# Two adjacency products as pairs of 64-row matmuls into two PSUM banks

## The chip, the cores and the metric

The kernel runs on one core of a Trainium2 chip. The metric is the device time of one execution in microseconds. Three runs of the kernel before are the base: 1310.28, 1312.41 and 1313.22 us, median 1312.41.

## What is computed

Four graph layers act one after the other on x, which has 8 batches, 2048 nodes and 64 features (f32). Each ends in `x = layernorm(x + layer(x))` over the 64 features. All of them use one adjacency matrix `adj` of 2048 x 2048, which is a symmetric 0/1 pattern whose rows are divided by their sums. The change touches the last two layers:

```python
# layer 2
out_self = jnp.einsum('bni,io->bno', x, weight_self)
x_neighbors = jnp.einsum('nm,bmi->bni', adj, x)
out_neighbors = jnp.einsum('bni,io->bno', x_neighbors, weight_neighbor)
return out_self + out_neighbors + bias
# layer 3
A_td = A + jnp.eye(n, dtype=A.dtype)
deg = jnp.sum(A_td, axis=1)
dinv = jax.lax.rsqrt(deg)
A_hat = dinv[:, None] * A_td * dinv[None, :]
H = jnp.einsum('bmd,nm->bnd', X, A_hat)
X_p = jnp.einsum('bnd,kd->bnk', H, W)
return X_p
```

Layer 0 is a polynomial in `adj` with weights of each node's own. Layer 1 mixes an adjacency product with attention over 64 groups.

## The kernel before

The 2048 nodes are 16 tiles of 128 partitions (NT = 16, P = 128). A row of a node holds all batches and features, 8 x 64 = 512 columns (BC). Since `adj` is a pattern times a scale of each row, layer 0 writes the pattern as exact zeros and ones ("masks") to DRAM, one block of 1 MB for each tile of output nodes. `cols_of` holds the scales for each node: `s1` for layer 2 and `sdinv` for layer 3.

**A product.** An adjacency product of output tile j is 16 steps over the input tiles mt, each with the mask block as the stationary operand (128 rows by 128 columns) and 512 columns of input as the moving operand. The input is split in two, a high and a low part, each of which goes through TensorE in the one-pass type fp32r; so a step is two matmuls, and a tile is 32, all accumulated in one PSUM bank. `times_mask` (L1440, its matmul on L1442) issues the two matmuls of a step. `mask_tile` (L1434) loads a mask block by a DMA on SP's queue (L1437); the pool has three buffers (L1504).

**Layer 2** (loop on L1545). Layer 1 leaves the projected inputs as `y_hi` and `y_lo`, and x with the self term in `x2`. For each tile j:

- 32 matmuls into `acc` (L1547 to L1549), whose pool `acc2` has two buffers (L1506);
- `r = acc * s1 + x2` on VectorE, one `scalar_tensor_tensor` (L1551);
- the layer norm of r (helper `layernorm`, L132 to L155: two reductions and two more passes over 512 columns on VectorE, a square and a square root on ScalarE), whose result goes back into `x2`;
- for tile j - 1, `projected` (L1528): four 128 x 128 transposes on TensorE (`transpose`, L167, tile `tr_l` in the profile), their copy `xT` on VectorE (L1518), four plain f32 matmuls with W (L1532, tile `yp`), then `v_hi` on ScalarE (L1536), and `v_lo` and a new `x2` on VectorE (L1537, L1540).

**Layer 3** (loop on L1558). The same product with `v_hi` and `v_lo`, `r = acc * sdinv + x2` (L1564), the layer norm, and the output's DMA on ScalarE's queue (L1569).

**PSUM.** In these layers the pools are `acc2`, `tr2` and `mm2`, of two buffers each, one bank a buffer.

**What sets the order of the work.** In layers 0 and 1 the order on each engine is the order of the code: these parts stand in `program_order()` (L210). Layers 2 and 3 do not. There a scheduler, which works with estimated durations and takes the code's order as priority, orders the instructions of each engine when the program is built. In the profile of before one sees its work: the 32 products of a tile stand on TensorE as five ahead of `yp` and 27 behind it, though the code has `projected` between two whole products. On the chip each engine then takes its instructions in that order.

**64-row matmuls elsewhere.** Several places already use pairs of 64-row matmuls on partitions 0 to 63 and 64 to 127, with plain f32 operands: L1109 (tile `pp`, layer 0), L807 (`fc`, layer 1) and L872 (`u`, the projection that prepares layer 2). A plain f32 matmul appears in the profile as two instructions, an fp32r one as one.

Of the kernel before, what the change touches and what calls it, by code (L numbers as in the profile page):

```python
# [8 lines left out]
F32 = mybir.dt.float32  # L9
# [3 lines left out]
ALU = mybir.AluOpType  # L13
# [5 lines left out]
P = 128  # L19
NT = N // P  # L20
NQ, QW = 4, 512
NP = B // 2
BC = B * C
# [34 lines left out]
def r_(ap):  # L58
    return ap.bitcast(F32R)
# [3 lines left out]
def kernel(  # L63
# [28 lines left out]
    nc = tc.nc  # L92
# [18 lines left out]
    cols_of = {  # L111
        k: const.tile([P, NT], F32, tag=k, name=k)
        for k in ("s1", "s2", "sdeg", "dinv", "dinv2", "sdinv")
    }

    def buffer(pool, k, name, per=1):

        return Tiles(
            [pool.tile([P, BC], F32, tag=f"b{k}_{t}", name=f"{name}_{t}") for t in range(NT)], per
        )  # L120
# [11 lines left out]
    def layernorm(ln, r, dst, name, swap=False, mhalf=None):  # L132

        r3 = b_view(r)
        s = ln([P, B], "s", f"s_{name}")
        nc.vector.tensor_reduce(s, r3, AX.X, ALU.add)
        nc.vector.scalar_tensor_tensor(
            r3, bcast(s), -1.0 / C, r3, op0=ALU.mult, op1=ALU.add  # L140
        )
        sq = ln([P, BC], "sq", f"sq_{name}")
        nc.scalar.activation(sq, r, AF.Square, scale=C ** -0.5)
        var = ln([P, B], "var", f"var_{name}")
        nc.vector.tensor_reduce(var, b_view(sq), AX.X, ALU.add)
        rstd = ln([P, B], "rstd", f"rstd_{name}")
        if mhalf is not None:
            nc.vector.tensor_scalar(var, var, EPS, None, op0=ALU.add)
            nc.gpsimd.tensor_tensor(rstd, var, mhalf, ALU.pow)
        else:  # L150
            std = ln([P, B], "std", f"std_{name}")
            nc.scalar.activation(std, var, AF.Sqrt, bias=eps_t)
            nc.vector.reciprocal(rstd, std)
        if not swap:
            nc.vector.tensor_tensor(b_view(dst), r3, bcast(rstd), ALU.mult)  # L155
            return
        for bq in range(2):
            nc.vector.tensor_tensor(
                swapped(dst, bq),
                r[:, 4 * bq * C:4 * (bq + 1) * C].rearrange("p (h l c) -> p h l c", h=2, l=2),  # L160
                rstd[:, 4 * bq:4 * bq + 4].rearrange("p (h l o) -> p h l o", h=2, o=1)
                .to_broadcast([P, 2, 2, C]),
                ALU.mult,
            )

    def transpose(dst, src):
        nc.tensor.matmul(dst, src, ident, start=True, stop=True, is_transpose=True)  # L167
# [1214 lines left out]
    def short_program(top):  # L1382
# [49 lines left out]
        y_hi, y_lo = buffer(big, 0, "y_hi"), buffer(big, 1, "y_lo")  # L1432

        def mask_tile(pool, j, name):  # L1434

            a = pool.tile([P, NT, P], F32, tag="mj", name=f"mj_{name}_{j}")
            nc.sync.dma_start(a, masks[j])  # L1437
            return a

        def times_mask(acc, a, hi, lo, mt):  # L1440
            for part in (hi, lo):
                nc.tensor.matmul(  # L1442
                    acc, r_(a[:, mt, :]), r_(part[:, mt, :]),
                    start=mt == 0 and part is hi, stop=mt == NT - 1 and part is lo,
                )

        def ln_tiles(pool):
            return lambda shape, tag, name: pool.tile(shape, F32, tag=tag, name=name)
# [5 lines left out]
        with tc.tile_pool(name="l0", bufs=1) as l0, tc.tile_pool(  # L1454
            name="raw", bufs=4
# [10 lines left out]
            ps_acc = acc_st.enter_context(tc.tile_pool(name="fi", bufs=1, space=PSUM))  # L1466
# [3 lines left out]
            with tc.tile_pool(name="l0s", bufs=2) as l0s, tc.tile_pool(  # L1470
                name="trs0", bufs=2, space=PSUM) as ps_tr, tc.tile_pool(
                name="pps0", bufs=2, space=PSUM
# [5 lines left out]
                s1, dinv = cols_of["s1"], cols_of["dinv"]  # L1478
# [18 lines left out]
        x2, a_first = layer1(  # L1497
            own, wts, fcw_sb, fcb_sb, av_sb, fcg_sb, vecs, rden, hgr, aggp, agg_st, h_sb, y_hi,
            y_lo, mask_tile, times_mask, w2_sb, bias2_sb, ps_acc, early,
        )  # L1500
# [3 lines left out]
        with tc.tile_pool(name="mj2", bufs=3) as mjp, tc.tile_pool(  # L1504
            name="l2", bufs=2
        ) as l2p, tc.tile_pool(name="ylo", bufs=1) as ylop, tc.tile_pool(  # L1506
            name="acc2", bufs=2, space=PSUM
        ) as ps_acc, tc.tile_pool(name="tr2", bufs=2, space=PSUM) as ps_tr, tc.tile_pool(
            name="mm2", bufs=2, space=PSUM
        ) as ps_mm:  # L1510
            ln = ln_tiles(l2p)

            def x_transposed(x, j, name):
                tr = ps_tr.tile([P, NP, P], F32, tag="tr", name=f"tr_{name}")
                for pr in range(NP):
                    transpose(tr[:, pr, :], x[:, j, pr * P:(pr + 1) * P])
                xT = l2p.tile([P, NP, P], F32, tag="xT", name=f"xT_{name}")
                nc.vector.tensor_copy(xT, tr)  # L1518
                return xT


            v_hi = buffer(own, 0, "v_hi")
            v_lo01 = wts.tile([P, 2, BC], F32, tag="pm", name="v_lo01")
            v_lo = Tiles([v_lo01[:, t] for t in range(2)] + [
                ylop.tile([P, BC], F32, tag=f"b0_{t}", name=f"v_lo_{t}") for t in range(2, NT)
            ])

            def projected(j):  # L1528
                xT = x_transposed(x2, j, f"l3_{j}")
                mm = ps_mm.tile([P, BC], F32, tag="mm", name=f"yp_{j}")  # L1530
                for pr in range(NP):
                    nc.tensor.matmul(  # L1532
                        mm[:, pr * P:(pr + 1) * P], xT[:, pr, :], w3_sb, start=True, stop=True
                    )
                di = cols_of["dinv"][:, j:j + 1]
                nc.scalar.activation(r_(v_hi[:, j, :]), mm, AF.Copy, scale=di)  # L1536
                nc.vector.scalar_tensor_tensor(  # L1537
                    r_(v_lo[:, j, :]), mm, di, v_hi[:, j, :], op0=ALU.mult, op1=ALU.subtract
                )
                nc.vector.scalar_tensor_tensor(  # L1540
                    x2[:, j, :], mm, cols_of["dinv2"][:, j:j + 1], x2[:, j, :],
                    op0=ALU.mult, op1=ALU.add,
                )

            for j in range(NT):  # L1545
                a = mask_tile(mjp, j, "l2") if j else a_first
                acc = ps_acc.tile([P, BC], F32, tag="acc", name=f"a2_{j}")  # L1547
                for mt in range(NT):
                    times_mask(acc, a, y_hi, y_lo, mt)  # L1549
                r = l2p.tile([P, BC], F32, tag="r", name=f"r2_{j}")  # L1550
                nc.vector.scalar_tensor_tensor(  # L1551
                    r, acc, cols_of["s1"][:, j:j + 1], x2[:, j, :], op0=ALU.mult, op1=ALU.add
                )
                layernorm(ln, r, x2[:, j, :], f"l2_{j}")
                if j:
                    projected(j - 1)
            projected(NT - 1)
            for j in range(NT):  # L1558
                a = mask_tile(mjp, j, "l3")
                acc = ps_acc.tile([P, BC], F32, tag="acc", name=f"a3_{j}")  # L1560
                for mt in range(NT):
                    times_mask(acc, a, v_hi, v_lo, mt)
                r = l2p.tile([P, BC], F32, tag="r", name=f"r3_{j}")
                nc.vector.scalar_tensor_tensor(  # L1564
                    r, acc, cols_of["sdinv"][:, j:j + 1], x2[:, j, :], op0=ALU.mult, op1=ALU.add
                )
                o = l2p.tile([P, BC], F32, tag="o", name=f"o_{j}")
                layernorm(ln, r, o, f"l3_{j}")
                nc.scalar.dma_start(out[j * P:(j + 1) * P, :], o)  # L1569
# [549 lines left out]
    with ExitStack() as stack:  # L2119
        short_program(stack)  # L2120
# [53 lines left out]
```

## Time and profile before

| what | value |
|---|---|
| median of three runs | 1312.41 us |
| the profiled execution: span from first to last instruction | 1314.5 us (its only time in the profile) |
| mean granted TensorE clock over the span | 0.971 of full speed |
| TensorE matmul, weight load | 1253.7 us (95%), 1002.0 us (76%) |
| VectorE, ScalarE, GpSimd | 886.6, 377.9, 514.4 us |
| layer 2, stretch 1045 to 1184 us: matmul, VectorE busy | 139.0, 81.6 us, clock 1.00 |
| layer 3, stretch 1184 to 1303 us: matmul, VectorE busy | 119.0, 62.7 us, clock 1.00 |
| after the last product, 1303 to 1314.5 us: VectorE busy | 3.7 us |

PE is TensorE's matmul part, PEld its weight loads, DVE VectorE, ACT ScalarE, POOL GpSimd, SP the queue of most DMAs. Matmuls overlap each other in the pipeline, so a matmul's own duration (389 ns for an fp32r matmul of 512 columns) is longer than the distance from one start to the next. The distance is what counts for the time of a stage. "64*128 64x256" after a matmul means a stationary operand of 64 rows by 128 columns and a moving one of 64 rows by 256 columns.

### The profile page before, as it was taken

The page shows a single profiled execution, that of the slowest core. Times are in us where ns is not written, and L with a number is a line of the kernel's source. Part 1 is how long each engine was busy: PE and PEld are TensorE (multiplying, and loading weights), DVE is VectorE, ACT ScalarE, POOL GpSimd, SP SyncE. Part 2 cuts the span into 40 slices and gives each one's busy share as a digit, 9 for nine tenths or more (in the row PEclk, how much of TensorE's full clock was granted, in tenths as well). Part 3 has the DMA queues.
Part 4 walks back from the last instruction along what each step waited for, and adds up shares of the span by engine and source line. Part 5 has one row for each costly group of instructions (what it writes and reads, how often), then busy time and mean ns, then how long its engine had stood idle before and what let it go on. Part 6 is the DMA issues. An engine that isn't in the chain of part 4 may idle for free. (4 is left out here: it accounts for less than half of the span.)

```text
span 1314.5 us, 19978 instructions
## 1 busy us (share of the span) xinstructions
PE 1253.7 (95%) x7692; PEld 1002.0 (76%) x7692; DVE 886.6 (67%) x1596; ACT 377.9 (29%) x852; POOL 514.4 (39%) x418
## 2 busy tenths in 40 slices
PE   7999799999999999999998599999998899999996
PEld 6777578888888888888886367777766788888885
DVE  5455268888887777887673568877774666665544
ACT  3000001222222222222222356666664521111111
POOL 1000274555554555555411468888872600000000
PEclk9999799999999999999997689999998999999998
DMA  8877833323333333332352212223220133334541
GB/s 293 240 210 149 217 94 105 105 102 102 106 107 107 108 107 107 107 106 82 112 187 75 101 65 97 96 96 97 81 96 1 70 124 128 104 122 152 187 173 67
DMA packets 100792, 157.22 MB, mean 120 GB/s; under 512 B 12881, under 2 KB 64465, under 8 KB 94673
## 3 DMA queue, kind: packets, MB, share of 16 engines
q1 hardware_dynamic: 98208, 151.65, 35.8%
q10 hardware_dynamic: 2304, 4.20, 0.8%
q8 instruction: 63, 1.03, 0.3%
q0 software_dynamic: 176, 0.02, 0.1%
q14 instruction: 41, 0.33, 0.1%
HBM read 118.08 MB, written 37.76 MB: 119 GB/s over the span
## 5 line engine op out<-in xcount | busy, mean ns | idle before, releaser
L1120 DVE SCALAR_TENSOR_TENSOR r<-pp,emb_sb,r 128x256 f32<-128x256 f32 x512 | 247.2, 483 | 105.3 <-PE pp L1109 90.4
L1109 PE MATMUL pp<-w_sb,xT 64*128 64x256 f32 x1024 | 160.6, 390 | 1.8 <-DVE r L1120 1.8
L1109 PE MATMUL pp<-w_sb,y1T 64*128 64x256 f32 x1024 | 153.6, 376 | 0.0
L1109 PE MATMUL pp<-w_sb,y2T 64*128 64x256 f32 x1024 | 153.6, 376 | 0.0
L1058 POOL TENSOR_TENSOR r<-xs,bn 128x256 f32<-128x256 f32 x32 | 22.8, 732 | 245.5 <-issue 213.2
L492 PE MATMUL y1p<-x_hi,m 128*128 128x512 f32 x256 | 107.4, 420 | 7.1 <-ACT x_hi L438 7.1
L1109 PEld LDWEIGHTS pp<-w_sb,xT 64*128 64x128 f32 x1024 | 94.5, 186 | 19.7 <-issue 9.6
L1109 PEld LDWEIGHTS pp<-w_sb,y2T 64*128 64x128 f32 x1024 | 99.8, 187 | 10.8
L1109 PEld LDWEIGHTS pp<-w_sb,y1T 64*128 64x128 f32 x1024 | 99.8, 187 | 10.8
L492 PE MATMUL y1p<-x_lo,m 128*128 128x512 f32 x256 | 104.1, 407 | 0.0
L1072 PE MATMUL y2p<-y_hi,msk 128*128 128x512 f32 x256 | 103.0, 402 | 0.0
L1442 PE MATMUL ind<-y_hi,mj_l 128*128 128x512 f32 x240 | 101.7, 424 | 0.0
L1072 PE MATMUL y2p<-y_lo,msk 128*128 128x512 f32 x256 | 101.3, 396 | 0.0
L1442 PE MATMUL a<-v_hi,mj_l 128*128 128x512 f32 x256 | 100.1, 392 | 0.0
L1442 PE MATMUL a<-v_lo,mj_l 128*128 128x512 f32 x256 | 100.0, 391 | 0.0
L1442 PE MATMUL a<-y_lo,mj_l 128*128 128x512 f32 x240 | 95.1, 396 | 0.0
L1442 PE MATMUL a<-y_hi,mj_l 128*128 128x512 f32 x240 | 94.9, 395 | 0.0
L1442 PE MATMUL ind<-y_lo,mj_l 128*128 128x512 f32 x240 | 94.6, 394 | 0.0
L739 POOL TENSOR_TENSOR ez<-ez,coef 128x1024 f32<-128x1024 f32 x32 | 69.9, 2183 | 56.3 <-DVE ez L737 54.9
L1011 POOL TENSOR_TENSOR ms<-msk,srow 128x1024 f32<-128x1024 f32 x32 | 89.8, 2806 | 4.7 <-DVE ms L1027 4.7
L1003 DVE TENSOR_SCALAR msk<-adj 128x1024 fp32r<-128x1024 f32 x32 | 63.6, 2021 | 9.1 <-DMA adj<-in_at 9.0
L492 PEld LDWEIGHTS y1p<-x_hi,m 128*128 128x128 f32 x256 | 50.2, 196 | 19.6 <-ACT x_hi L438 7.1
(286 smaller groups left out, 2430.3 us busy)
## 6 DMA issues: line engine op xcount, KB each, us to landing
mj_l<-mask SPq DMA_DIRECT2D x46, 1024.0 KB, 4.9
raw<-in_at SPq DMA_DIRECT2D x32, 512.0 KB, 5.0
adj<-in_at SPq DMA_DIRECT2D x64, 256.0 KB, 3.9
mask<-msk SPq DMA_DIRECT2D x32, 512.0 KB, 4.6
xraw<-in_xn SPq DMA_DIRECT2D x8, 512.0 KB, 4.6
oh<-oh SPq DMA_DIRECT2D x32, 128.0 KB, 2.8
xT<-in_xt SPq DMA_DIRECT2D x16, 256.0 KB, 3.2
xs<-in_xn SPq DMA_DIRECT2D x16, 256.0 KB, 2.9
```

The costliest lines, as they stand in the source:

```text
L492: nc.tensor.matmul(accs[q][jj], r_(m[:, t, jj * P:(jj + 1) * P]), r_(part[:, mt, :]), start=i + h + t == 0 and part is x_hi, stop=i == 3 a ...
L739: nc.gpsimd.tensor_tensor(by_b(ez), by_b(ez), per_b(coef, 2 * i, 2), ALU.mult)
L1003: nc.vector.tensor_scalar(r_(m), raws[j][h], 0.0, None, op0=ALU.is_gt)
L1011: nc.gpsimd.tensor_tensor(ms, m, srow[j].unsqueeze(1).to_broadcast([P, 8, P]), ALU.mult)
L1058: nc.gpsimd.tensor_tensor(r[:, 4 * bq * C:4 * (bq + 1) * C] .rearrange("p (h l c) -> p h l c", h=2, l=2), swapped(terms[j]["xs"], bq), bn. ...
L1072: nc.tensor.matmul(acc, r_(msk[j, mt // 8][:, mt % 8, :]), r_(part[:, mt, :]), start=mt == 0 and part is y_hi, stop=mt == NT - 1 and part ...
L1109: nc.tensor.matmul(pp[:, h, pl, :], terms[j][name][rs, 2 * bq + pl], w_sb[rs, k, dq * 4 * C:(dq + 1) * 4 * C], start=k == 0, stop=k == K - 1,)
L1120: nc.vector.scalar_tensor_tensor(rb, ppv[:, :, dd, :], emb_sb[:, j, d:d + 1], rb, op0=ALU.mult, op1=ALU.add)
L1442: nc.tensor.matmul(acc, r_(a[:, mt, :]), r_(part[:, mt, :]), start=mt == 0 and part is hi, stop=mt == NT - 1 and part is lo,)
```

## The change

`product` replaces the loop over `times_mask` in layers 2 and 3. Each matmul over 128 rows becomes two: one over partitions 0 to 63 of both operands, which accumulates in the first of two PSUM banks, and one over partitions 64 to 127, which accumulates in the second. `acc` grows from one bank to two. `scaled_sum` replaces the one VectorE operation on `acc` by two: the first takes the first bank times the scale plus x, the second the second bank times the scale plus the result of the first. Layers 0 and 1 and the projection are as before.

```diff
+            def product(a, hi, lo, name):
+
+                acc = ps_acc.tile([P, 2, BC], F32, tag="acc", name=name)
+                for mt in range(NT):
+                    for part in (hi, lo):
+                        for h in range(2):
+                            rs = slice(h * 64, (h + 1) * 64)
+                            nc.tensor.matmul(
+                                acc[:, h, :], r_(a[rs, mt, :]), r_(part[rs, mt, :]),
+                                start=mt == 0 and part is hi, stop=mt == NT - 1 and part is lo,
+                            )
+                return acc
+
+            def scaled_sum(acc, scale, x, name):
+
+                r = l2p.tile([P, BC], F32, tag="r", name=name)
+                for h in range(2):
+                    nc.vector.scalar_tensor_tensor(
+                        r, acc[:, h, :], scale, r if h else x, op0=ALU.mult, op1=ALU.add
+                    )
+                return r
...
             for j in range(NT):
                 a = mask_tile(mjp, j, "l2") if j else a_first
-                acc = ps_acc.tile([P, BC], F32, tag="acc", name=f"a2_{j}")
-                for mt in range(NT):
-                    times_mask(acc, a, y_hi, y_lo, mt)
-                r = l2p.tile([P, BC], F32, tag="r", name=f"r2_{j}")
-                nc.vector.scalar_tensor_tensor(
-                    r, acc, cols_of["s1"][:, j:j + 1], x2[:, j, :], op0=ALU.mult, op1=ALU.add
-                )
+                acc = product(a, y_hi, y_lo, f"a2_{j}")
+                r = scaled_sum(acc, cols_of["s1"][:, j:j + 1], x2[:, j, :], f"r2_{j}")
                 layernorm(ln, r, x2[:, j, :], f"l2_{j}")
...
                 a = mask_tile(mjp, j, "l3")
-                acc = ps_acc.tile([P, BC], F32, tag="acc", name=f"a3_{j}")
-                for mt in range(NT):
-                    times_mask(acc, a, v_hi, v_lo, mt)
-                r = l2p.tile([P, BC], F32, tag="r", name=f"r3_{j}")
-                nc.vector.scalar_tensor_tensor(
-                    r, acc, cols_of["sdinv"][:, j:j + 1], x2[:, j, :], op0=ALU.mult, op1=ALU.add
-                )
+                acc = product(a, v_hi, v_lo, f"a3_{j}")
+                r = scaled_sum(acc, cols_of["sdinv"][:, j:j + 1], x2[:, j, :], f"r3_{j}")
```

## The prediction

> **What bounds the kernel now.** I read the page first, for the engines' totals and the chain of waits; then the chain in order of time over layers 2 and 3; then the timeline there; and last the timeline of places that already use 64-row matmuls. From the page:
>
> ```profile
> span 1314.5 us, 19978 instructions
> PE 1253.7 (95%) x7692; PEld 1002.0 (76%) x7692; DVE 886.6 (67%) x1596; ACT 377.9 (29%) x852; POOL 514.4 (39%) x418
> ...
> PE a L1442 18%; PE ind L1442 9%; PE fc L807 3%; PE df L816 2%; PE gp L707 1%; PE yp L1532 1%; PE trm L167 1%; PE red L748 1%; PE dp L727 1%; PE pp L1109 1%; PE tr_l L167 1%; PE ind L1275 0%; PE u L872 0%; DVE ez L737 0%; DVE d L717 0%
> ```
>
> The products that the diff touches are "a L1442", 18% of the span and all of it on the chain. The chain in order of time (start, us, engine, what), one tile of layer 2, then the end of layer 3:
>
> ```profile
> 1068.63 0.44 PE tr_l L167 x4
> 1069.06 1.17 PE a L1442 x5
> 1070.23 1.07 PE yp L1532 x8
> 1071.29 6.16 PE a L1442 x27
> ...
> 1192.39 111.11 PE a L1442 x486
> 1303.53 0.76 DVE r L1564
> ```
>
> TensorE ends both stages. A tile of layer 2 lasts 0.44 + 1.17 + 1.07 + 6.16 = 8.84 us. In layer 3 a matmul comes every 111.11 / 486 = 0.2286 us, and I call that a slot; 1024 slots make up the two layers. VectorE is busy 81.6 of 139.0 us in layer 2 (the stretch from 1045 to 1184) and 62.7 of 119.0 in layer 3. It bounds neither, but it ends one wait in each tile (timeline: start, us, engine, line):
>
> ```profile
> 1059.62 0.60 PE L167 MATMUL tr_l<-ident,x 128*128 128x128 f32 x4
> ...
> 1059.90 0.75 DVE L1551 SCALAR_TENSOR_TENSOR r<-a,s,x 128x512 f32<-128x512 f32 x1 [1.76 <-PE a L1442]
> ...
> 1060.57 0.68 DVE L1518 COPY xT_l<-tr_l 128x512 f32<-128x512 f32 x1
> ...
> 1061.30 0.97 PEld L1532 LDWEIGHTS yp<-w_sb,xT_l 128*128 128x128 f32 x8 [0.35 <-DVE xT_l L1518]
> 1061.30 1.16 PE L1532 MATMUL yp<-w_sb,xT_l 128*128 128x128 f32 x8
> ```
>
> The copy xT_l stands behind r on VectorE, and the matmuls yp wait for the copy: 5.5 us over 16 tiles. The five matmuls "a" between tr_l and yp are what the scheduler put there to cover it.
>
> **What the Trainium skill says.** (1) "TensorE: Matmul & The Clock Gate", Part 3, The mechanism: matmuls in different row groups run at the same time, starting some 4 ns apart. This trace agrees for plain f32 (below); no 64-row pair here is fp32r, as the products are. (2) The same page, LDWEIGHTS: a load costs by its columns, not by its rows. It agrees: 187 ns for 64x128 (L1109), 188 ns for 128x128 (L1442). (3) The same page, Back-to-back issue gap: 216 ns for 512 columns. The trace has 228.6 where the weights change with every matmul. (4) "TensorEngine Tiling (Array Packing)", Key Properties: a change of tiling mode drains TensorE. It agrees, with a price worked out below.
>
> **The change, part by part.** First the pairs. The places with 64 rows beside those with 128 rows (each f32 matmul is two instructions, so fc x4 is two pairs and u x16 is eight):
>
> ```profile
> 980.58 1.02 PE L748 MATMUL red<-ez,ST 128*128 128x512 f32 x2
> ...
> 1001.72 1.13 PE L807 MATMUL fc<-sT,fcw_sb 64*128 64x512 f32 x4 [0.82 <-ACT sT L799]
> ...
> 1036.69 1.16 PE L872 MATMUL u<-w_sb,xT 64*128 64x128 f32 x16
> 1037.78 0.66 PE L167 MATMUL tr<-ident,x 128*128 128x128 f32 x4
> 1038.36 1.16 PE L872 MATMUL u<-w_sb,xT 64*128 64x128 f32 x16
> ```
>
> Eight pairs of 64x128 take 1.16 us; eight single 128x128 (yp above) take 1.16 us. Two pairs of 64x512 take 1.13; two singles 1.02. So the halves do run together, and a pair costs what one full matmul costs: no less. That is also what I expect by reasoning: both halves start and end together, so whatever makes a slot 228.6 instead of 216 happens in both at once. *Products: 1024 pairs in place of 1024 matmuls, 0 us.* Bounds: if a pair takes 216 (the skill's gap; also the pace of L1109, where a group of four of 256 columns comes every 0.432 us), 1024 x 12.6 ns = -12.9; if the 7 ns by which the second half of an L1109 pair starts later are added to each slot, +7.2.
>
> Second, the changes of tiling mode. The transposes tr_l (L167) and yp (L1532) stay 128-row, so each tile of layer 2 now switches four times: a, tr_l, a, yp, a. The price comes from the cycle u, tr, u above: 1038.36 - 1036.69 = 1.67 us. In it stand eight pairs and four transposes, whose single starts in the trace lie 0.112 and 0.109 apart once they run: 0.90 and 0.44. The rest is 0.33 for two switches, 0.17 each. In L1109 the first pair after another mode starts 0.093 late and lasts 0.104 longer, its load being bare; for the way back to the products I use 0.19. Four switches are 0.72 per tile. Of the wait at yp about 0.17 is then covered: 0.55 per tile net, if the copy xT_l is not later.
>
> Third, the second VectorE operation. r now takes two operations of 0.75 in place of one, and xT_l is queued behind both: it comes some 0.70 later, and so does yp. If only five slots stand between tr_l and yp, a tile pays 0.70 plus 0.19 for the switch back, 0.89. Nothing else queued behind it matters: x2 of a tile (the last one: r at 1183.52, x at 1189.67) was ready 6.15 us after r began, and its transpose starts a whole tile, 8.8 us, later. The scheduler will see the longer wait and put some three more matmuls there. If it prices a 64-row one like a full one, the eight are four slots: 0.70 + 0.19 + 0.23 = 1.12. I cannot see which; I take 0.80, between 0.55 and 1.12. *Layer 2: 16 x 0.80 = 12.8 us* (8.8 to 17.9).
>
> Fourth, the start of layer 3. x of the last tile was ready at 1189.67 and tr_l took it at 1189.83, so the added operation delays it: *+0.75* (0 to 2, by how many products the scheduler puts ahead). Layer 3 itself has no other switch; r there lies beside the next product.
>
> Fifth, the tail: the last r is on the chain with nothing beside it; a dependent operation starts 0.79 after the one before (1303.53, 1304.32): *+0.79*. The second PSUM bank costs nothing: acc2 takes four banks, tr2 and mm2 two each, eight in all, and each acc still has two buffers. The loads double in number, but two of 187 ns run together in different row groups as in L1109. The mask transfers land in 4.9 us with three buffers, well within a product: 0.
>
> Sum: 0 + 12.8 + 0.75 + 0.79 = +14.3 on a span of 1314.5, 1328.8. The profile gives no other time for that execution; its span is 2.1 above the median of 1312.4, and I carry the difference: 1328.8 - 2.1 = **1326.7 us**.
>
> **The rivals.** *Faster pairs (the other side).* A pair takes 216: -12.9. With the switches at their least (8.8) and 1.5 for the ends the sum is -2.6: 1309.8. It decides from a slot of 218.4 down (10.3 us over 1024); with my 12.8 it would take 214.6, less than any pace here. For it: the paces of L1109 and of the skill. Against: u against yp, fc against red. *Half slots.* The scheduler puts five 64-row matmuls, two and a half slots, ahead of yp: 0.70 + 0.19 + 2.5 x 0.229 = 1.46 per tile, 23.4 + 1.5 = +24.9: 1337.3. For it: before, it came out 0.35 short. Against: it must see r's second operation. *No overlap.* fp32r halves run one after the other, so that the change doesn't do what it says: 1024 x 0.2286 = 234 more, some 1560. Against: every f32 pair here overlaps; for it: no fp32r pair is seen.
>
> **How the numbers follow.** Likeliest, pairs as slots: 0.60, 1317 to 1338 (slots of 224 to 233). Faster pairs: 0.22 (0.10 faster, 0.10 within, 0.02 slower, by the switches). Half slots 0.12, no overlap 0.06. Of the likeliest 0.02 falls within. So faster 0.10, within 0.2% 0.12, slower 0.78; 0.2%, 2.6 us, is about what a measurement of this kernel can tell from no change. The range leaves out no overlap, the half of the faster pairs that gains, and a tip above half slots: 1310 to 1340.
>
> **What would show it.** Right: layer 3's products still take about 0.229 per pair; tr_l and yp each begin and end with a gap of some 0.17 to 0.2; a tile of layer 2 lasts near 9.6 us; the last r is two operations. Wrong: a pair of 216 or less in layer 3, or 450; no gaps at tr_l and yp; an unchanged wait for xT_l.

## The result and the profile after

The changed kernel takes 1328.24 us (median of four runs, 1327.99 to 1331.94) against 1312.55 before (1310.28 to 1313.22). By the medians it is slower by 15.7 us. The ratio of the means is 1.013, 95% interval 1.0116 to 1.0145, which is 17.0 us. The forecast was 1326.7, 14.3 us slower.

The page of the changed kernel, with the lines that answer to those of before:

```profile
span 1326.7 us, 22058 instructions
PE 1264.1 (95%) x8716; PEld 1016.2 (77%) x8716; DVE 911.1 (69%) x1628; ACT 379.4 (29%) x852; POOL 513.2 (39%) x418
...
PE a L1529 18%; PE ind L1442 9%; PE fc L807 3%; PE df L816 2%; PE gp L707 1%; PE yp L1554 1%; PE trm L167 1%; PE red L748 1%; PE dp L727 1%; PE pp L1109 1%; PE tr_l L167 1%; PE u L872 0%; PE ind L1275 0%; DVE ez L737 0%; DVE d L717 0%
```

The products are now "a L1529": 1024 more matmuls, and still 18% of the span. The totals tell nothing of the cause. The chain in order of time does (start, us, engine, what; one tile of layer 2, then the passage into layer 3 and its end):

```profile
1066.16 0.59 PE tr_l L167 x4
1066.75 0.89 PE a L1529 x5
1067.64 0.03 issue
1067.67 1.16 PE yp L1554 x8
1068.83 7.04 PE a L1529 x59
...
1199.91 0.70 DVE xT_l L1518
1200.62 0.04 issue
1200.66 1.16 PE yp L1554 x8
1201.82 113.90 PE a L1529 x995
1315.72 0.02 issue
1315.74 0.76 DVE r L1539
1316.51 0.02 issue
1316.53 0.76 DVE r L1539
```

Layer 3 first: 995 matmuls are 497.5 pairs, and 113.90 / 497.5 = 0.2289 us a pair. Before, a full matmul took 0.2286. A pair costs a slot, no more and no less. A tile of layer 2, from one tr_l to the next, went from 8.83 to 9.71 us. There are five 64-row matmuls ahead of yp and 59 behind it, where there were five full ones and 27. Five is odd: the third pair is torn apart by yp. Its first half runs alone ahead of yp; behind yp its second half runs beside the first half of the next step, and so on, until the last half of the tile is alone again. So the 64 halves take 33 slots in place of 32.

The timeline at the same place (start, us, engine, line):

```profile
1066.09 0.66 PE L167 MATMUL tr_l<-ident,x 128*128 128x128 f32 x4
1066.27 0.75 DVE L1539 SCALAR_TENSOR_TENSOR r<-a,s,x 128x512 f32<-128x512 f32 x1 [3.05 <-PE a L1529]
...
1066.94 0.68 DVE L1518 COPY xT_l<-tr_l 128x512 f32<-128x512 f32 x1
...
1067.53 0.74 DVE L1539 SCALAR_TENSOR_TENSOR r<-a,s,r 128x512 f32<-128x512 f32 x1
1067.67 0.97 PEld L1554 LDWEIGHTS yp<-w_sb,xT_l 128*128 128x128 f32 x8 [0.47 <-DVE xT_l L1518]
```

The copy xT_l does not stand behind both operations on r, as the prediction had it. The scheduler put it between them, and yp starts 1.58 us after tr_l (before: 1.68).

In numbers, from the start of the first product of layer 2 to the start of the last matmul of layer 3, the profile of before has 258.1 us (1044.98 to 1303.11) and that of after 273.7 (1041.63 to 1315.32): +15.6. It divides into 0.1 in the first two products, 14 tiles x 0.877 = 12.3 in layer 2, 3.0 at the start of layer 3, and 0.0 to 0.2 in the rest of layer 3. The start of layer 3 is worked out so: from the second last tr_l to the end of the last yp 9.28 us against 8.88, in which 14.5 slots of layer 3 were done against 26; 0.4 + 11.5 x 0.2287 = 3.0. At the last tr_l TensorE now waits for the layer norm (timelines of before and of after):

```profile
1189.83 0.63 PE L167 MATMUL tr_l<-ident,x 128*128 128x128 f32 x4
```

```profile
1199.25 0.63 PE L167 MATMUL tr_l<-ident,x 128*128 128x128 f32 x4 [1.74 <-DVE x L155]
```

The tail comes on top. From the first operation on the last r (1303.53 and 1315.74) to the end of the last operation on VectorE, the chains of before and of after have 4.94 and 5.73 us, +0.79:

```profile
1307.78 0.69 DVE o L155
```

```profile
1320.78 0.69 DVE o L155
```

The profile thus accounts for 16.4 us, between the 15.7 of the medians and the 17.0 of the means. The whole time from the last matmul to the end does not show the 0.79: after the last VectorE operation, the profiled execution of before needed 6.1 us to its end, that of after 5.3, and the other kernels 4.9 to 5.4.

The two spans differ by only 12.2 us, because the profiled execution of before came to layer 2 3.35 us later, in work that the change does not touch.

### The profile page after: what moved, and what is told of

Its sections match the earlier page's. It is cut to its first block, busy times and chain, and to the rows that moved or that the text cites. A ratio compares the mean times of both kernels' runs of the same rounds, so it can differ in the third digit from the quotient of the medians.

```text
span 1326.7 us, 22058 instructions
## 1 busy us (share of the span) xinstructions
PE 1264.1 (95%) x8716; PEld 1016.2 (77%) x8716; DVE 911.1 (69%) x1628; ACT 379.4 (29%) x852; POOL 513.2 (39%) x418
## 5 line engine op out<-in xcount | busy, mean ns | idle before, releaser
L1529 PE MATMUL a<-v_hi,mj_l 64*128 64x512 f32 x512 | 117.9, 388 | 0.0
L1529 PE MATMUL a<-v_lo,mj_l 64*128 64x512 f32 x512 | 117.6, 388 | 0.0
L1529 PE MATMUL a<-y_hi,mj_l 64*128 64x512 f32 x480 | 116.0, 397 | 0.0
L1529 PE MATMUL a<-y_lo,mj_l 64*128 64x512 f32 x480 | 112.2, 390 | 0.0
L1109 PEld LDWEIGHTS pp<-w_sb,y2T 64*128 64x128 f32 x1024 | 99.8, 187 | 10.8
L1529 PEld LDWEIGHTS a<-v_hi,mj_l 64*128 64x128 f32 x512 | 93.9, 184 | 5.6 <-issue 0.3
L1529 PEld LDWEIGHTS a<-v_lo,mj_l 64*128 64x128 f32 x512 | 93.8, 184 | 5.0
L1529 PEld LDWEIGHTS a<-y_hi,mj_l 64*128 64x128 f32 x480 | 82.9, 184 | 12.5 <-issue 2.4
```

The source lines that it names most:

```text
L1109: nc.tensor.matmul(pp[:, h, pl, :], terms[j][name][rs, 2 * bq + pl], w_sb[rs, k, dq * 4 * C:(dq + 1) * 4 * C], start=k == 0, stop=k == K - 1,)
L1529: nc.tensor.matmul(acc[:, h, :], r_(a[rs, mt, :]), r_(part[rs, mt, :]), start=mt == 0 and part is hi, stop=mt == NT - 1 and part is lo,)
```

## The experiments

The theory at this point: a pair is a slot, and the loss is around the 128-row matmuls (switches of tiling mode; a pair torn apart; too little work in front of a wait). The rivals: pairs are in themselves longer (15 ns each would make 15.7 us), or VectorE's second operation is what costs. "Rest" below is the time from the first product of layer 2 to the end of the span in the profile, "tile" the median time from one tr_l to the next in layer 2. In rest, before is some 0.7 to 1.1 us too long, by its late end.

| kernel | median us | ratio to before (95%) | rest us | tile us |
|---|---|---|---|---|
| before (median in the groups of runs) | 1311.4 to 1312.8 | | 269.6 | 8.830 |
| the changed kernel | 1328.2 | 1.0130 (1.0116 to 1.0145) | 285.1 | 9.707 |
| l2_only | 1323.6 | 1.0086 (1.0073 to 1.0099) | 280.4 | 9.686 |
| l3_only | 1316.0 | 1.0028 (1.0017 to 1.0038) | 272.3 | 8.831 |
| head3 | 1326.5 | 1.0106 (1.0091 to 1.0121) | 283.4 | 9.484 |
| head5 | 1323.8 | 1.0080 (1.0067 to 1.0093) | 280.2 | 9.373 |
| switch_64 | 1323.0 | 1.0093 (1.0076 to 1.0111) | 278.9 | 8.831 |
| no_switch_128 | 1316.2 | 1.0031 (1.0018 to 1.0045) | 272.6 | 8.831 |
| two_ops | 1313.0 | 1.0008 (1.0000 to 1.0016) | 269.1 | 8.831 |
| head7 | 1309.8 | 0.9981 (0.9972 to 0.9990) | 266.0 | 8.631 |
| tr64 | 1327.5 | 1.0135 (1.0114 to 1.0156) | 284.4 | 9.686 |
| tr64_head5 | 1321.2 | 1.0060 (1.0047 to 1.0073) | 275.6 | 9.067 |
| head5_start | 1321.4 | 1.0073 (1.0057 to 1.0090) | 278.5 | 9.373 |
| half_l3 | 1312.7 | 1.0010 (1.0001 to 1.0018) | 269.2 | 8.831 |

**Which layer: l2_only and l3_only.** The change in one of the two layers; the other has full matmuls, into one bank of the same two-bank tile.

```diff
-                acc = product(a, v_hi, v_lo, f"a3_{j}")
-                r = scaled_sum(acc, cols_of["sdinv"][:, j:j + 1], x2[:, j, :], f"r3_{j}")
+                acc = ps_acc.tile([P, 2, BC], F32, tag="acc", name=f"a3_{j}")[:, 0, :]
+                for mt in range(NT):
+                    times_mask(acc, a, v_hi, v_lo, mt)
...
```

This is l2_only, where layer 3 has its single operation on r again; l3_only does the same to layer 2 in place of layer 3.

> Pairs in layer 2 alone; layer 3 has full matmuls again. Theory (switches of tiling mode around tr_l and yp, and one slot lost per tile because the odd fifth 64-row matmul ahead of yp runs alone): nearly all of the loss stays, 14 tiles x 0.87 us = 12.2 and a few tenths at the start of layer 3, so +12 to +13.5 us on before. Rival (a pair is in itself longer than a full matmul, 15.7 us / 1024 = 15 ns each): half of the loss, +8 us. Rival (the second VectorE operation on r is what costs): about half too, +7 to +9 us.

> Pairs in layer 3 alone. Theory: no switches inside layer 3, so only the start of layer 3 (up to 3 us, the scheduler puts too little work ahead of the last tile's transposes) and the tail of 0.8 us: +2 to +4 us. Rival (longer pairs): +8 us, and a distance of some 0.243 us between pairs in the trace instead of 0.229. Rival (second VectorE operation): +7 to +9 us.

Layer 2 alone keeps +11.4 us (the profile's rest: +10.8), a little less than expected; layer 3 alone +3.8 (rest: +2.7). From the first product to the last matmul, where the late end of before does not count, it is +12.0 and +3.1. The layers hold the same number of pairs, so the pairs are not what costs, nor are the VectorE operations. Nor is the tile of two banks: in l3_only, layer 2 has it with full matmuls, and its tile is 8.831. In layer 3 alone the 998 matmuls after the last yp take, by the chain of l3_only:

```profile
1188.09 114.15 PE a L1529 x998
```

114.15 / 499 = 0.2288: the rival "longer pairs", which wanted 0.243, is out.

**The torn pair: head3 and head5.** Three or five whole pairs of the next product are written ahead of yp; otherwise the changed kernel.

```diff
-            def projected(j):
+            def projected(j, ahead=None):
                 xT = x_transposed(x2, j, f"l3_{j}")
+                if ahead is not None:
+                    ahead()
...
-                    projected(j - 1)
+                    projected(j - 1, lambda: ahead(j + 1, 3))
```

(`ahead(j, n)` issues the next n pairs of product j; the loop issues what is left of it. head5 has 5 in place of 3.)

> The changed kernel, but three whole pairs (six 64-row matmuls) stand between tr_l and yp instead of five 64-row matmuls; nothing else is moved in layer 2. Theory: the slot lost by the split pair comes back, 14 x 0.229 = 3.2 us: 1325 us. Rivals (longer pairs, or VectorE): no difference to the changed kernel, 1328 us.

> The changed kernel with five whole pairs between tr_l and yp, as many slots as before the change. Theory: the 3.2 us of the split pair, and the wait of yp for xT_l (0.1 us beyond the switch in each tile) is covered too, 1.4 us: 1323.5 us; the four switches (0.65 us a tile net, 9 us) stay, so it is still about 0.8% slower than before. Rivals: 1328 us (longer pairs); VectorE: 1323 or less with no gap left at tr_l.

The chains of head3 and of head5, one tile each:

```profile
1066.04 0.59 PE tr_l L167 x4
1066.63 0.89 PE a L1579 x6
1067.52 0.04 issue
1067.56 1.16 PE yp L1556 x8
1068.72 6.81 PE a L1579 x58
```

```profile
1066.35 0.59 PE tr_l L167 x4
1066.94 1.36 PE a L1579 x10
1068.29 1.09 PE yp L1556 x8
1069.38 6.34 PE a L1579 x54
```

In head3 six matmuls take the 0.89 us that five took: the sixth is free, beside the fifth. The tile falls by 9.707 - 9.484 = 0.223, one slot, as expected. The time shows less of it: 1.8 us by the medians and 1.7 by rest, of 3.2 expected. In the profiled execution of head3 the granted clock was 0.59 from 1199 to 1202 us, at the start of layer 3, where it was 1.00 in head5 and in the changed kernel; from the second last tr_l on, TensorE needed 1.6 us more than in the changed kernel. Why is not shown. In head5 the "issue" step ahead of yp is gone as well: the copy xT_l ends 0.41 us before yp starts, and the tile falls by another 0.111. What is left over before is 9.373 - 8.830 = 0.543 us a tile with no wait for xT_l and no torn pair in it.

**The price of a switch: switch_64 and no_switch_128.** The kernel before, with one small matmul more in the middle of each product of layer 3, of 64 rows or of 128; its output is read by nothing.

```diff
                 for mt in range(NT):
+                    if mt == 8:
+                        ex = ps_tr.tile([P, NP, P], F32, tag="tr", name=f"ex_{j}")
+                        nc.tensor.matmul(
+                            ex[:, 0, :], ident[0:64], ident[0:64], start=True, stop=True
+                        )
                     times_mask(acc, a, v_hi, v_lo, mt)
```

> The kernel before with one extra plain f32 matmul of 64 rows (identity by identity, into a spare PSUM tile that nothing reads) in the middle of each of the 16 products of layer 3: two switches of tiling mode per tile. Theory: two drains of 0.09 and two bare loads of 0.06 to 0.10 us beside its own 0.11 to 0.13 us: 16 x (0.12 + 0.35) = 7.5 us more than before, and 4.5 to 6 us more than the same with 128 rows. Rival (no price for a switch; it is the pairs or VectorE that cost): the same as with 128 rows.

> The same extra matmul with all 128 rows, so that no tiling mode changes. Theory and rival: 16 x (0.22 us for its two passes) = about 3.5 us or less more than before; the layer-3 products keep their 0.229 us.

The timelines of TensorE around one such matmul, first with 64 rows, then with 128:

```profile
1217.21 0.39 PE L1442 MATMUL a<-v_lo,mj_l 128*128 128x512 f32 x1
1217.53 0.49 PE L1564 MATMUL ex<-ident 64*128 64x128 f32 x2
1217.94 0.50 PE L1442 MATMUL a<-v_hi,mj_l 128*128 128x512 f32 x1
1218.28 0.39 PE L1442 MATMUL a<-v_lo,mj_l 128*128 128x512 f32 x1
```

```profile
1210.13 0.39 PE L1442 MATMUL a<-v_lo,mj_l 128*128 128x512 f32 x1
1210.36 0.38 PE L1564 MATMUL ex<-ident 128*128 128x128 f32 x2
1210.50 0.48 PE L1442 MATMUL a<-v_hi,mj_l 128*128 128x512 f32 x1
1210.82 0.39 PE L1442 MATMUL a<-v_lo,mj_l 128*128 128x512 f32 x1
```

From the product's matmul ahead to the second one behind: 1.07 us against 0.69. Fewer rows, and 0.38 longer. By the profile's rest it is 278.9 - 272.6 = 6.3 us for 32 switches, 0.20 each; by the medians 6.8, 0.21 each. The change of mode has a price where no pair and no second operation is present. The expectation had it a little too low: switch_64 was to cost 7.5 us over before, and cost 10.8.

**VectorE alone: two_ops.** The kernel before, with a second operation on r in both layers, which adds 0.0 x acc.

```diff
+                nc.vector.scalar_tensor_tensor(r, acc, 0.0, r, op0=ALU.mult, op1=ALU.add)
```

> The kernel before with a second VectorE operation on each r that reads acc again times 0.0 and adds r (the result stays): the VectorE part of the change alone, full matmuls. Theory: only the tail, +0.8 us, and up to 0.7 at the start of layer 3: 1313 to 1314. Rival of the prediction's third step (xT_l comes 0.7 us later in each tile of layer 2 and yp waits for it): +10 to +11 us, 1323.

+0.8 us, interval 0.0 to 2.1; the tile stays at 8.831, and yp's waits for xT_l are the 5.5 us of before. The second operation lies beside other work everywhere but in the tail. At the start of layer 3 the last tr_l comes 0.70 us later, but three more matmuls of layer 3 stand ahead of it, and from the first product to the last matmul two_ops takes 258.1 us like before.

**The switches taken out: tr64, then tr64_head5.** The transposes as 64-row pairs too, which leaves two switches in a tile.

```diff
-                    transpose(tr[:, pr, :], x[:, j, pr * P:(pr + 1) * P])
+                    for h in range(2):
+                        rs = slice(h * 64, (h + 1) * 64)
+                        nc.tensor.matmul(
+                            tr[:, h, pr, :], x[rs, j, pr * P:(pr + 1) * P], ident[rs, rs],
+                            start=True, stop=True, is_transpose=True,
+                        )
```

> The changed kernel with the transposes of layers 2 and 3 made 64-row pairs as well (two banks, one buffer); yp stays 128-row. So two of the four switches in each tile go. Theory: a switch is worth 0.195 us (from the two kernels with the extra matmul), so 2 x 0.195 x 16 = 6.2 us less than the changed kernel, 1322; a tile period of 9.3 us in place of 9.71. Rival (the transposes themselves grow as pairs, or VectorE's strided copy): 1326 to 1328.

A miss: 1327.5, and a tile of 9.686. The chain shows why:

```profile
1064.47 0.75 DVE r L1545
1065.22 0.61 DVE xT_l L1524
1065.82 0.04 issue
1065.87 1.16 PE yp L1560 x8
1067.03 7.04 PE a L1535 x59
```

With two and a half slots ahead of yp, the tile is set by VectorE: the product's end, the first operation on r, the copy xT_l, yp. TensorE without the switches only waits longer for it (yp waited 17.6 us for xT_l in all, 7.6 in the changed kernel). So in the changed kernel the switches around tr_l and the wait lie beside each other, and taking out the switches alone gains nothing. Five whole pairs in front should bring the switches into view:

> 64-row transposes and five whole pairs ahead of yp together. The 64-row transposes alone gained nothing, where yp waited 0.70 us for xT_l in each tile; the question is whether the two switches cost nothing, or were hidden under that wait. Theory (hidden under the wait): with five whole slots in front the two switches show, so the tile period falls from 9.37 us (five pairs alone) to about 9.1, and the time by 14 x 0.28 = 3.9 us, to about 1320. Rival (the 64-row transposes and the strided copy cost as much as the two switches): a period of 9.37, 1323.8.

The tile fell to 9.067, by 0.31, and the rest by 4.6 us against head5; the medians differ by 2.6, each against its own runs of before by 3.2. TensorE around the transposes, in head5 and in tr64_head5:

```profile
1065.96 0.39 PE L1579 MATMUL a<-y_lo,mj_l 64*128 64x512 f32 x2
1066.28 0.66 PE L167 MATMUL tr_l<-ident,x 128*128 128x128 f32 x4
...
1067.20 0.40 PE L1579 MATMUL a<-y_lo,mj_l 64*128 64x512 f32 x2
```

```profile
1065.52 0.39 PE L1585 MATMUL a<-y_lo,mj_l 64*128 64x512 f32 x2
1065.75 0.40 PE L1519 MATMUL tr_l<-ident,x 64*128 64x64 f32 x8
...
1066.28 0.39 PE L1585 MATMUL a<-y_lo,mj_l 64*128 64x512 f32 x2
```

From the pair ahead to the second pair behind it is 0.76 us in place of 1.24. Not all of this is the switches, since the transposes changed too: their moving operand has 64 columns in place of 128. With full matmuls and the transposes of before, the same stretch takes 0.90. So 0.34 is the two switches, and 0.14 the shorter transposes. At yp some 0.14 was lost again, since it starts 0.06 us after the end of xT_l, where in head5 it starts 0.41 after: a remnant of the wait is left.

**The start of layer 3: head5_start.** head5, and 19 pairs of layer 3's first product ahead of the last tile's transposes, where the changed kernel has 20 64-row matmuls, ten pairs' worth.

```diff
+            first = product3(0)
+            projected(NT - 2, lambda: on(first, 5))
+            on(first, 19)
+            projected(NT - 1, lambda: on(first, 5))
+            on(first, 2 * NT)
```

> The kernel with five whole pairs ahead of yp, and besides 19 whole pairs of layer 3's first product ahead of the last tile's transposes, in place of 11. Theory: the wait of TensorE for the last layer norm at the start of layer 3 (1.7 us and more in the changed kernel) goes: some 2 to 2.7 us less than with five pairs alone, 1321. What is then left over before is the switches, 16 x 0.55 = 8.8 us, and the tail of 0.8. Rival: the wait only moves to yp or to v_hi, no gain, 1323.5.

1321.4, 2.4 below head5; each against its own runs of before, the difference is 1.6, and the intervals overlap (rest: 1.7). TensorE no longer waits for the last layer norm at tr_l, but the product now runs out before v_hi of the last tile is made: the chain of head5_start goes through v_hi (0.70) and v_lo (0.76). Part of the wait went, and part moved, as the rival had it for all of it.

What the scheduler put ahead of the last yp can be counted in six kernels. The three numbers are matmuls of layer 3's first product ahead of the second last yp, from there to the last tr_l, and from there to the last yp:

| kernel | matmuls of layer 3 | operations on r in layer 2 | ahead of the last yp |
|---|---|---|---|
| before | 128 rows | one | 5 + 17 + 4 = 26 |
| half_l3 (below), l3_only | 64 rows | one | 5 + 17 + 4 = 26 |
| two_ops, l2_only | 128 rows | two | 5 + 20 + 4 = 29 |
| the changed kernel | 64 rows | two | 5 + 20 + 4 = 29 |

The second operation adds three matmuls, and a 64-row matmul counts like a full one: in pairs, 29 are 14.5 slots.

**One half alone: half_l3.** l3_only with `range(1)` for h: the second half of every sum in layer 3 is left out.

> Layer 3 alone in 64-row matmuls, and only the first half of each pair: the second half of every sum in layer 3 is left out, so it computes half of layer 3's product. Theory (halves of a pair run together, and a half alone costs what a full matmul costs): layer 3 keeps 0.227 to 0.229 us a slot, the time is that of before within 1 to 2 us. Rival (pairs are partly serial, the second half costs something): a shorter slot than 0.227 and a time below before.

The 486 matmuls of the chain's last stretch, 64 rows each:

```profile
1191.62 111.21 PE a L1529 x486
```

111.21 / 486 = 0.2288, the same as for 128 rows and for a pair. Half of the rows saves nothing; the second half, in the other row group, costs nothing. Between the first product and the last matmul half_l3 takes 0.8 us more than before, all of it at the start of layer 3, where its 64-row matmuls meet the transposes and yp: switches again, with 26 slots ahead as before, no pair and one operation on r.

**A version that beats both: head7.** The kernel before, full matmuls, with seven of them ahead of yp in place of five.

> The kernel before with seven full matmuls instead of five between tr_l and yp. Theory: the wait for xT_l (0.18 us a tile with the bare load behind it) is covered: 14 x 0.18 = 2.5 us less than before, 1310; the tile period falls from 8.83 to 8.65 us. Rival: yp's load is bare in any case, so only 0.08 a tile, 1311.

1309.75 us, ratio 0.9981 (0.9972 to 0.9990): 2.4 us faster than before. Its chain:

```profile
1066.72 0.44 PE tr_l L167 x4
1067.15 1.61 PE a L1555 x7
1068.77 0.89 PE yp L1534 x8
1069.66 5.69 PE a L1555 x25
```

yp takes 0.89 in place of 1.07, the last of the wait and the bare load behind it being gone. The waits for xT_l, 5.5 us in the profile of before, are 0.6, and were worth 2.4. The tiles alternate between 8.63 and 8.68; 32 slots and the 1.33 us of transposes and yp are 8.65, so next to nothing is left to cover there.

## Why the prediction was right, and where it was not

**Products, 0 us: right.** 0.2289 a pair for 0.2286 a matmul. The reason given, that both halves start and end together, is not needed. In layer 2 of head5 the halves of a pair do start 3 to 4 ns apart. In layer 3 of the changed kernel, behind a torn pair, the second half of one step runs beside the first half of the next, mostly 20 to 33 ns apart, and the pace is the same. half_l3 shows it for one half alone. Why it is 0.229, and not the 0.216 that the Trainium skill gives as the isolated gap of a matmul ("TensorE: Matmul & The Clock Gate", Back-to-back issue gap), was not tried. Two slips in the working change nothing: it counts instructions where it says pairs (fc x4 is one pair of f32 matmuls), and the 218.4 of the rival comes out as 218.5.

**Switches, 0.72 a tile, 0.55 net: right.** Measured from the matmul of the product ahead to the second one behind, the transposes take 1.237 us in head5 and 0.902 in before, and yp 1.738 in head5 and 1.355 in head7, neither of which waits for xT_l. So the four switches cost 0.335 + 0.383 = 0.718. In before yp takes 1.532, so 0.177 of wait was there to be covered, where the prediction had 0.17. head5 shows the net, 0.543; switch_64 gives 0.20 for one switch. The two of a group are not alike, as the prediction had them: ahead of the 128-row matmuls it is 0.08, behind them the rest. And the longer first matmul behind, which it puts down to a bare load, is hardly part of the price: to the next start it takes 0.34 us in switch_64, but 0.32 in no_switch_128 too, where no mode changes.

**"xT_l is queued behind both: it comes some 0.70 later": wrong.** The scheduler set the copy between the two operations, and yp came no later. The place where the prediction looked was right, though: the chain r, xT_l, yp decides the tile as soon as too few slots stand in front (tr64).

**Half slots: this rival's mechanism came, with another price.** The scheduler did leave five 64-row matmuls ahead of yp. The prediction gave that case 0.12 and 1.46 us a tile. It cost 0.223 for the torn pair and 0.111 for the wait. With the switches, 0.543 + 0.223 + 0.111 = 0.877 a tile against the 0.80 taken. (These are the shares in the order in which head3 and head5 took them away; tr64 shows that another order gives others.) The size was met by a mean between two cases, of which neither was what happened. That was luck.

**Start of layer 3, 0.75: the wrong mechanism, and mis-sized.** The measured 3.0 holds the last two of the 16 tiles too, for which the prediction had booked 2 x 0.80. So 2.35 stands against 3.0. The 0.75 itself was to be the delay of the last layer norm by the second operation. But two_ops has that delay and pays nothing, since the scheduler put 29 matmuls ahead in place of 26. What costs is that in the changed kernel these 29 are 14.5 slots: TensorE ran out of them and waited 1.74 us at the last tr_l. The half-slot thought was applied to the tiles and forgotten here.

**Tail, 0.79: right.** The second operation starts 0.79 after the first (1315.74, 1316.53), and the last VectorE operation ends 5.72 to 5.73 us after the first one on r in all kernels with pairs in the whole of layer 3, 4.93 to 4.94 in those with one operation.

**The 2.1 us carried from span to median: the wrong reading of a right number.** The later arrival of that one execution at layer 2, not something around the span, made it longer; after's span lies 1.7 below that run's own time. The forecast difference, 14.3, does not depend on it.

The two other rivals are out by measurement: faster pairs (in layer 3 the next half but one never starts less than 0.224 us later), and no overlap (a pair takes 0.2289, not twice 0.2286).

## What to carry to other kernels

Splitting a matmul that already fills 128 rows into two 64-row halves gains no time even when the halves run together perfectly: the pace of 512 columns was the same for 128 rows, for a pair and for one half. What it adds are switches around every group of 128-row matmuls in between, 0.17 to 0.20 us each here, and a scheduler that takes a half for a whole, as this one did, covers its waits with half of the work that it means to put there. Before one prices a switch, one should see what the engine would wait for without it: in this kernel removing two switches gained nothing until the wait beside them was covered.

## What the runs showed of the hardware

- A one-pass fp32r matmul of 512 columns came every 0.2286 to 0.2289 us on average in each of three forms: 128 rows (before), two halves in two row groups (after), one half alone (half_l3).
- A small matmul of 64 rows between 128-row matmuls cost 0.38 us more than one of 128 rows in the same place (switch_64, no_switch_128).
- Two 64-row halves in different row groups ran beside each other also when they belonged to different steps of the product (after, layer 3).
